# Issuing the first store behind a group of loads with 13 fields still outstanding

## Chip, core and metric

The kernel runs on one core of a Trainium2 chip. The metric is device time in microseconds for one execution of the whole program; lower is better.

## What is computed

For each of 4096 samples, x holds 32 fields of 64 numbers, and W is a 64 x 64 matrix. Each field is multiplied by W, and every pair of fields i < j (496 pairs) gives an elementwise product:

```python
vid = jnp.einsum('bfd,de->bfe', x, W)
F_ = x.shape[1]
idx_i, idx_j = jnp.triu_indices(F_, k=1)
return x[:, idx_i, :] * vid[:, idx_j, :]
```

All is 32-bit floating point. The output is 15 times as large as the input: the profile counts 33.59 MB read from HBM and 520.09 MB written to it.

## The kernel before

**Tiles.** Samples are split into 16 tiles of 256. A tile lies in on-chip memory with the 64 embedding numbers on the partitions, two halves of the samples on the lower and the upper 64 of them, and 32 fields of 128 samples along each partition. One field of a tile is thus 128 partitions x 512 bytes, 64 KB. On-chip memory is one tensor, `mem`, of 445 such fields, and both input tiles and outgoing products have places in it: `XPLACE` says where each tile lies, `SLOTS` the size and place of each of the 71 store buffers. Many places are used again and again, so a load or a product must wait until the store that reads the place has finished.

**Work on a tile.** TensorE computes `vid` for the 32 fields into PSUM (L173). VectorE multiplies the fields with broadcast fields of `vid` (L197), in blocks of pairs, and writes the products into the buffer of the moment. When a buffer is full, SP issues one DMA that stores it (L200).

**Loads.** Tile 0 comes first, in two DMAs (L137, L141). Then follow, at the head of the program, tiles 1 to 3 in one DMA and tiles 5 and 4 in two. Two more groups of five tiles each are loaded in the course of the program: tiles 6 to 10, and tiles 15 to 11. The loop asks for them when two loaded tiles are left. `GROUPS` names the tiles, `CUTS` the pieces into which a group's load is cut, as ranges of fields within it:

```python
CUTS = [[None, [(0, 32), (32, 64)]], [(0, 127), (127, 160)], [(33, 160), (0, 33)]]
```

**Order.** Everything that SP does stands in one queue, in the order in which the program names it; loads and stores alike go out on it. A DMA is cut into 128 rows, one for each partition, and these are spread over 16 DMA engines, eight rows to each.

**The extra wait.** `load` returns the list of DMAs of the pieces, and `pieces` holds the latest list. The first store that comes after a group of loads gets a dependency, set by `behind`, so that SP issues it only when an earlier piece has landed. With `pieces.pop(0)` this is the first piece of the list, which leaves 32 fields of load outstanding at the head and 33 in the two middle groups. After that store `pieces` is empty, and later stores wait for VectorE alone. This wait is no matter of correctness: the store reads other places than the load writes.

Of the kernel before, what the change touches and what calls it, by code (L numbers as in the profile page):

```python
# [21 lines left out]
    [[6, 7, 8, 9, 10]],  # L22
    [[15, 14, 13, 12, 11]],
]
CUTS = [[None, [(0, 32), (32, 64)]], [(0, 127), (127, 160)], [(33, 160), (0, 33)]]
XPLACE = [317, 349, 381, 413, 32, 0, 285, 317, 349, 381, 413, 128, 96, 64, 32, 0]


# [25 lines left out]
def by_block():  # L54


    def within(lo):
        yield "step", lo, 2, 1, 0
        for k in range(2):
            yield "step", lo, 4, 2, k  # L60
        for i in (lo, lo + 8):
            yield "row", i + 4, i, 4, 4
        yield "row", lo + 8, lo, 8, 8

    yield from within(0)
    yield "row", 16, 0, 16, 16
    yield from within(16)


def products(blocks, at=0):  # L70

    for kind, a, b, c, d in blocks:
        if kind == "row":
            rows, n, i0, di, j0, dj = c, d, b, 0, a, 1
        else:
            rows, n, i0, di, j0, dj = 16 // b, c, a, b, a + c + d, b
        r = k = 0
        while r < rows:
            room = BREAKS[bisect_right(BREAKS, at)] - at
            if k or room < n:  # L80
                m, w = 1, min(n - k, room)
            else:
                m, w = min(rows - r, room // n), n
            yield at, m, w, i0 + r * di + k, di, j0 + r * dj, dj
            at += m * w
            if k + w == n:
                r, k = r + m, 0
            else:
                k += w
# [10 lines left out]
@with_exitstack  # L100
def pairwise_bilinear_kernel(
    ctx: ExitStack,
    tc: tile.TileContext,
    x0: bass.AP,
    x: bass.AP,
    out: bass.AP,
):

    nc = tc.nc
    NT = sum(len(tiles) for group in GROUPS for tiles in group)
    F = x0.shape[1] - 1 - PAD0
    D = P // 2
    NP = F * (F - 1) // 2

    BANK = 512 // C


    ctx.enter_context(tc.manual_schedule(engines={mybir.EngineType.SP}))

    const = ctx.enter_context(tc.tile_pool(name="const", bufs=1))
    psum = ctx.enter_context(
        tc.tile_pool(name="ps", bufs=1, space=bass.MemoryType.PSUM)
    )
    vid = psum.tile([P, F, C], F32)

    mem = const.tile([P, UNITS, C], F32)  # L130


    w2 = const.tile([P, D], F32)


    place = XPLACE[0]
    nc.sync.dma_start(  # L137
        out=mem.rearrange("p u c -> p (u c)")[:, place * C - D : (place + F // 2) * C],
        in_=x0.rearrange("p u c -> p (u c)")[:, C - D : (1 + F // 2) * C],
    )  # L140
    nc.sync.dma_start(out=mem[:, place + F // 2 : place + F, :], in_=x0[:, 1 + F // 2 : 1 + F, :])  # L141
    nc.vector.tensor_copy(w2, mem[:, place - 1, C - D :])  # L142
    loaded = 1

    def load(tiles, cuts=()):
        nonlocal loaded
        n = len(tiles) * F
        place = XPLACE[tiles[0]]
        at = (loaded - 1) * F
        loaded += len(tiles)  # L150
        return [
            nc.sync.dma_start(out=mem[:, place + lo : place + hi, :], in_=x[:, at + lo : at + hi, :])  # L152
            for lo, hi in cuts or [(0, n)]
        ]

    ready = mybir.DependencyInfo(mybir.DependencyClass.Sync, mybir.DependencyReason.DATA)

    def behind(later, earlier):
        tc.add_manual_dep(later.ins, earlier.ins.name, ready, reason="issued when that has landed")

    pieces = []
    groups, cuts = iter(GROUPS), iter(CUTS)
    for tiles, parts in zip(next(groups)[1:], next(cuts)):
        pieces = load(tiles, parts)

    for t in range(NT):
        xt = mem[:, XPLACE[t] : XPLACE[t] + F, :]


        for b in range(0, F, BANK):  # L170
            for h in range(2):
                half = slice(h * D, (h + 1) * D)
                nc.tensor.matmul(  # L173
                    vid[half, b : b + BANK, :],
                    lhsT=w2[half, :],
                    rhs=xt[half, b : b + BANK, :],
                    start=True,
                    stop=True,
                )

        for at, m, w, i, di, j, dj in products(by_block(), t * NP):
            slot = bisect_right(STARTS, at) - 1
            n = m * w
            begin, end = STARTS[slot], STARTS[slot + 1]
            ot = mem[:, SLOTS[slot][1] : SLOTS[slot][1] + SLOTS[slot][0], :]
            o = ot[:, at - begin : at - begin + n, :]
            if m == 1:
                left = xt[:, i : i + w, :]
                right = vid[:, j : j + 1, :].to_broadcast([P, w, C])
            else:  # L190
                o = o.rearrange("p (m w) c -> p m w c", m=m)
                right = vid[:, j : j + (m - 1) * dj + 1 : dj, :].unsqueeze(2).to_broadcast([P, m, w, C])
                if di == 0:
                    left = xt[:, i : i + w, :].unsqueeze(1).to_broadcast([P, m, w, C])
                else:
                    left = xt.rearrange("p (m d) c -> p m d c", d=di)[:, i // di : i // di + m, i % di : i % di + w, :]
            nc.vector.tensor_tensor(o, left, right, ALU.mult)  # L197
            at += n
            if at == end:
                store = nc.sync.dma_start(out=out[:, begin:end, :], in_=ot)  # L200
                if pieces:
                    behind(store, pieces.pop(0))
                    pieces.clear()


        if t + 2 == loaded < NT:
            (tiles,) = next(groups)
            pieces = load(tiles, next(cuts))
# [45 lines left out]
```

## Time and profile before

| | |
|---|---|
| median of three runs | 1288.03 us (1287.9 to 1288.14) |
| profiled execution, its own time | 1287.86 us |
| its span, first to last instruction | 1286.1 us |
| VectorE busy with products (L197) | 1091.0 us, 455 instructions |
| TensorE busy (L173) | 220.7 us, 512 instructions |
| VectorE idle, waiting for stores | 154.9 us |
| TensorE idle, waiting for loads | 89.5 us, three times |
| stores (L200) | 71; 19.7 to 41.7 us from issue to landing, median 25.5 |
| loads of groups (L152) | 7; 21.3 to 44.3 us from issue to landing, median 37.8 |

The span is what the profile shows; the execution's own time has 1.76 us around it. The shares of busy time are averages, and busy time of an engine that isn't the bound costs nothing. In a list of waits a line reads: who waited, for whom, microseconds in total, times, longest. In a table of windows each line is a stretch of time, the busy time of TensorE's multiplications, its weight loads, VectorE and GpSimd with the number of their instructions, the clock granted to TensorE, the DMA engines' busy share, and GB/s. There a row of a transfer is counted where it starts, so the rates of short stretches scatter.

### The profile page before, as it was taken

Reading aid. Unit: us, or ns where it says so; the run is one execution under the profiler, and the core shown is the slowest. Engines: PE = TensorE matmul, PEld = TensorE weight load, DVE = VectorE, ACT = ScalarE, POOL = GpSimd, SP = SyncE. Lnnn points to the kernel's source line nnn. Section 1 sums busy time; section 2 is a strip of 40 time slices with the busy share of each in tenths; the row PEclk is TensorE's granted clock in tenths of the full one; section 3 lists DMA queues with packets and bytes.
Section 4 is the critical chain, followed back from the end, with each engine's and each line's share of the span. In section 5 each row is a group of like instructions: output and inputs, shape, how many; then the busy total and the mean of one; then the engine's idle time right before and its main releaser. Section 6 shows DMA issues by size and latency. Waiting matters only on the chain.

```text
span 1286.1 us, 1756 instructions
## 1 busy us (share of the span) xinstructions
PE 220.7 (17%) x512; PEld 40.5 (3%) x512; DVE 1091.2 (85%) x456; POOL 0.2 (0%) x4
## 2 busy tenths in 40 slices
PE   4031221303110113030311211103121120212000
PEld 1000000000000000000000000000000000000000
DVE  6899979988995489998998995649999799999952
POOL 0000000000000000000000000000000000000000
PEclk8555565555555656555655655555555565656555
DMA  9999999999999999999999999999999999999998
GB/s 385 434 433 440 442 424 443 431 437 428 432 442 421 441 425 433 434 441 428 434 433 443 426 437 427 417 443 428 431 434 445 423 441 435 421 447 421 445 423 376
DMA packets 11529, 553.79 MB, mean 431 GB/s; under 512 B 1280, under 2 KB 1280, under 8 KB 1280
## 3 DMA queue, kind: packets, MB, share of 16 engines
q1 hardware_dynamic: 11520, 553.69, 99.7%
q8 instruction: 4, 0.07, 0.0%
q14 instruction: 5, 0.04, 0.0%
HBM read 33.59 MB, written 520.09 MB: 431 GB/s over the span
## 4 chain that ended last, share of the span: by engine, by line
DMA 48%; DVE 47%; issue 3%; PE 0%; DVEq 0%; SPq 0%
DVE mem L197 47%; DMA out_dram<-mem 44%; DMA mem<-in_r_x_dram 3%; PE vid L173 0%; DVEq L242 0%; DVEq L197 0%; SPq L200 0%; DVE w L142 0%; SPq L152 0%
## 5 line engine op out<-in xcount | busy, mean ns | idle before, releaser
L197 DVE TENSOR_TENSOR mem<-mem,vid 128x1024 f32<-128x1024 f32 (+16 forms) x455 | 1091.0, 2471 | 164.8 <-DMA out_dram<-mem 154.9
L173 PE MATMUL vid<-mem,w 64*64 64x512 f32 x512 | 220.7, 985 | 963.3 <-DVE mem L197 867.7
L173 PEld LDWEIGHTS vid<-mem,w 64*64 64x64 f32 x512 | 40.5, 196 | 1141.9 <-DVE mem L197 1010.5
L142 DVE COPY w<-mem 128x64 f32<-128x64 f32 x1 | 0.2, 195 | 5.9 <-DMA mem<-in_r_x_dram 5.9
L222 POOL MEMSET const-bfloat16-1.0<- 128x1 bf16 x1 | 0.1, 101 | 0.0
L222 POOL MEMSET const-uint8-127<- 128x1 uint8 x1 | 0.1, 101 | 0.0
L222 POOL MEMSET const-float32-0.0<- 128x1 f32 x1 | 0.1, 98 | 0.2 <-issue 0.2
L222 POOL MEMSET const-float32-1.0<- 128x1 f32 x1 | 0.1, 98 | 0.0
## 6 DMA issues: line engine op xcount, KB each, us to landing
out_dram<-mem SPq DMA_DIRECT2D x21, 8128.0 KB, 26.7
out_dram<-mem SPq DMA_DIRECT2D x13, 7936.0 KB, 28.4
out_dram<-mem SPq DMA_DIRECT2D x3, 7424.0 KB, 24.8
out_dram<-mem SPq DMA_DIRECT2D x3, 6656.0 KB, 22.4
out_dram<-mem SPq DMA_DIRECT2D x3, 6144.0 KB, 21.0
out_dram<-mem SPq DMA_DIRECT2D x3, 5888.0 KB, 23.9
out_dram<-mem SPq DMA_DIRECT2D x3, 5440.0 KB, 24.6
mem<-in_r_x_dram SPq DMA_DIRECT2D x2, 8128.0 KB, 38.1
```

Source lines behind the costliest of these rows:

```text
L142: nc.vector.tensor_copy(w2, mem[:, place - 1, C - D :])
L173: nc.tensor.matmul(vid[half, b : b + BANK, :], lhsT=w2[half, :], rhs=xt[half, b : b + BANK, :], start=True, stop=True,)
L197: nc.vector.tensor_tensor(o, left, right, ALU.mult)
L222: nc = _bacc.Bacc("TRN2", target_bir_lowering=False, num_devices=1, dynamic_dma_scratch_size=1024)
```

## The change

The groups' loads are cut differently. The head's two pieces are 51 and 13 fields instead of 32 and 32. The middle groups are loaded in three pieces instead of two: 127, 20 and 13 fields, and the same sizes counted from the other end for the last group. The first store behind a group of loads waits for the last piece but one, so that 13 fields are outstanding when it is issued. What is loaded, where it goes, and all the computation stay as they are.

```diff
-CUTS = [[None, [(0, 32), (32, 64)]], [(0, 127), (127, 160)], [(33, 160), (0, 33)]]
+CUTS = [[None, [(0, 51), (51, 64)]], [(0, 127), (127, 147), (147, 160)], [(33, 160), (13, 33), (0, 13)]]
...
                 store = nc.sync.dma_start(out=out[:, begin:end, :], in_=ot)
                 if pieces:
-                    behind(store, pieces.pop(0))
+                    behind(store, pieces[-2])
                     pieces.clear()
```

## The prediction

> **What bounds the kernel now.** I read the page from the top, then SP's own waits, SP's timeline around the loads, and the rates in windows. The page first:
>
> ```profile
> span 1286.1 us, 1756 instructions
> PE 220.7 (17%) x512; PEld 40.5 (3%) x512; DVE 1091.2 (85%) x456; POOL 0.2 (0%) x4
> ...
> DMA  9999999999999999999999999999999999999998
> ...
> q1 hardware_dynamic: 11520, 553.69, 99.7%
> ...
> HBM read 33.59 MB, written 520.09 MB: 431 GB/s over the span
> ```
>
> The 16 DMA engines are busy in every slice, so the transfers bound the kernel. Section 4's chain gives 47% to VectorE, but it ends in stores and each VectorE stretch in it lies beside a full queue: VectorE itself waits 154.9 us for stores to free their buffers. A microsecond that an engine of the DMA loses is therefore a microsecond of the end, if that engine is the last one. SP's waits show where the change acts:
>
> ```profile
> SPq L200 <- DVE mem L197: 1109.7, 67, 34.7
> SPq L200 <- DMA mem<-in_r_x_dram: 97.6, 3, 36.9
> ```
>
> Of 71 stores (L200), three wait for a load. They are these, each the first store row behind a row of loads (L152) in SP's timeline:
>
> ```profile
> 1.62 1.65 SPq L152 DMA_DIRECT2D mem<-in_r_x_dram  x3
> 27.90 15.13 SPq L200 DMA_DIRECT2D out_dram<-mem  x2
> ...
> 382.50 1.56 SPq L152 DMA_DIRECT2D mem<-in_r_x_dram  x2
> 420.32 0.82 SPq L200 DMA_DIRECT2D out_dram<-mem  x2
> ...
> 790.47 1.64 SPq L152 DMA_DIRECT2D mem<-in_r_x_dram  x2
> 829.05 2.72 SPq L200 DMA_DIRECT2D out_dram<-mem  x2
> ```
>
> At the head, the rate of the transfers falls once that store has been issued (last column, GB/s):
>
> ```profile
> 22.50:29.00 6.50, 5.28 (x14) 1.41 (x16) 6.50 (x5) 0.00 (x0) 0.61 0.99 423
> 29.00:32.50 3.50, 0.80 (x4) 0.00 (x0) 3.50 (x1) 0.00 (x0) 0.78 1.05 290
> ...
> 100.00:380.00 280.00, 52.13 (x112) 8.19 (x108) 260.94 (x114) 0.00 (x0) 0.52 1.00 435
> ```
>
> 290 instead of 423 GB/s, with the engines busy all the time: the last load packets run slower while the store is queued behind them. The packet records say the same: rows of 16 KB take 0.61 us until 29.1 us and up to 1.48 us after it, and the store's rows follow each engine's last load row about 10 ns later. There is no hole now.
>
> What the view can't show is how far the 16 engines are apart. I took it from the 16 completion updates of each transfer. All engines carry the same rows, but at the end the first is done at 1281.78 us and the last at 1285.27 us. The last engine sets the time.
>
> **What the Trainium skill says.** "DMA: Bandwidth & Descriptors", section "Queues, rings and completion order": an issuing sequencer has one ring on each of 16 engines, consumed in order. The trace agrees (10 ns from row to row, store after load). The same page, "Why a DMA increments its semaphore by 16 and not by 1": only the full 16 means that all has landed. The trace agrees: the first load at 382.50 landed on its engines from 418.21 to 420.27 us, and the waiting store went out at 420.32. The same page, "Specifications", gives 0.6 us from issue to the first byte on this path. The trace shows more: the first load is issued at 0.73 and its rows start, engine by engine, from 1.72 to 2.41 us, so 1.0 to 1.7 us. I use the trace.
>
> **The change part by part.** Call L the time from SP's issue of the store to its first row. It is not seen on a drained queue. From below, the start of the program shows 1.0 us. The slowdown sets in 1.2 us after the issue at the head, and 1.4 us at 829.05. From above: at 420.32 the first engine out of load rows started the store's row at 422.88 without a hole, so at most 2.55 us. I take 1.5 and keep 1.1 and 2.55 for the range.
>
> *Two more transfers.* The middle groups are loaded in three pieces instead of two; the head keeps its number. From the medians of rows (16,384 B 0.611 us, 8,192 B 0.309 us), a row costs 0.007 us plus its bytes at 27.1 GB/s, and a 0.01 us gap. Eight more rows per engine are 0.14 us, twice 0.28 us, on the path. SP's own issue (0.34 to 1.25 us for one) hides in its 37 us wait.
>
> *Who waits.* Behind the waiting store stand only stores: at 420.72 (already computed) and 831.43, and at the head one at 42.69. The wait grows by 19 fields at the head, some 3 us, and by 20 in the middle; the queue is full in that time. TensorE's data comes with the untouched first piece in the second group (127 fields) and the third (33 to 160); tile 4, split at the head, is used far later. VectorE waits for landings of stores, which move with the queue. No cost, and what little it is late (0 to 1 us) VectorE's 165 us of idle time covers.
>
> *The tail.* After the wait, 13 fields are left: 8 x (0.007 + 6,656 B / 27.1 GB/s + 0.01) = 2.1 us, against 5.0 us now. From landing to issue takes 0.05 to 0.08 us, and a row's end to its landing 0.34 us. So the store comes 0.4 + L = 1.9 us behind the slowest engine's last row of the piece, just before its tail is over (2.1). A slowest engine has no hole while L stays below 1.7. A faster one has: its lead + 1.9 - 2.1.
>
> *Head.* The two pieces land on the slowest engine at 27.82 and 34.08: 6.26 us for 8 x 0.622 = 4.98, so 1.28 lost; the mean (27.34 to 33.48) loses 1.16. After: the slowest ends its loads at 34.08 - 1.28 - 0.34 = 32.46; the store comes at 32.46 - 2.1 + 1.9 = 32.26. Engines are only 0.8 apart here. Gain 1.25 us for the slowest, about 0.8 for the mean.
>
> *First middle join.* Slowest 420.27 to 426.27: 6.00 for 8 x 0.64 = 5.12, 0.88 lost. Mean 418.86 to 423.98: nothing lost, only late engines are hit. After: 420.27 - 1.25 + 5.12 + 0.14 - 0.34 = 423.94 is the slowest's end, and the store starts on every engine at 423.7 to 423.9. Now they start it from 422.88 to 425.99, mean 423.6. The slowest gains 2.05 in all, but the leads of the others, up to 3.1 us, are gone: they wait for the slowest, as at a barrier.
>
> *Second.* Those leads matter, because single engines are held up: comparing the updates of successive stores, one engine loses 1.44 us near 167, one 1.45 near 489, one 1.96 near 788 (and gets 0.53 back), one 1.76 near 1115 us, and none of the last three was the slowest. With leads gone, such a loss counts in full. An undelayed engine takes 403.78 us from the first join to the next load (423.24 to 827.02, the first updates); from 423.94 + 0.34 this gives 828.06, and with 1.43 of delay 829.5, against 828.99 now. Loads end at 829.5 + 5.12 + 0.14 - 0.34 = 834.4 and all start there; now from 831.71 to 834.92. Gain left: 0.5 us.
>
> *To the end.* Undelayed 449.69 us (832.09 to 1281.78). From 834.4 + 0.34: 1284.43. The engine that loses 1.76 gains some 1.3 on the mean: 1285.7, against 1285.27. **Sum: +0.4 us**, so the profiled execution goes from 1287.86 (span 1286.1 and 1.76 around it) to 1288.3. The median is 0.17 above that execution: 1288.4.
>
> The same sum engine by engine with L = 1.1 ends at -0.9, with 2.0 at +1.6, with 2.55 at +3.2 us.
>
> **Rivals.**
> 1. *Slow rows gone, leads not needed.* If delays belong to fixed slow engines, or fall on engines with room, the slowest saves 1.28 + 0.88 + 1.09 (828.99 to 835.20 is 6.21 for 5.12) - 0.28 = 3.0: 1285.1. For it: the engine last at 835 is still last at the end. Against: the engines delayed near 489, 788 and 1115 were others.
> 2. *A hole at each join.* With L near 2.5, even the slowest engine stands idle for 0.4 + 2.5 - 2.1 = 0.8 us at each of three joins, and the faster ones 2 to 3 us more, so that their later delays count in full: +3.2, 1291.2. For it: at 420.32 no row slowed before 2.4 us after issue. Against: 1.2 to 1.4 us at the other two. It decides from L = 2.3 on, at two or three joins.
> 3. *The slowdown belongs to the change of direction itself*, and hits the last load rows wherever the store is issued; 13-field rows are then slowed as the larger were, and only the two transfers count: 1288.3 + small holes, 1288.6. Against: onset follows the issue, not the end of the loads.
>
> **How the numbers follow.** Forecast 0.62, rival one 0.12, rival two 0.20, rival three 0.06. About 0.2%, or 2.6 us (1285.5 to 1290.6), is what a measurement of this kernel can tell from no change. Rival one lies mostly below it, so faster 0.10; rival two mostly above it, and a little of the forecast's upper bound, so slower 0.20; same 0.70. The range runs from part of rival one to rival two: 1285.9 to 1291.3.
>
> **What would show it.** Load rows keep their 0.61 us equivalent to the last one at the head, and the rate from 29 to 32.5 stays near 423. Two more DMA issues at L152. First stores at about 30.8, 422 and 832 us. The first rows of these stores start on all engines within 1 us of each other, with holes on the fast engines of 2 us in the middle. Wrong if the slow rows remain, if the engines keep their leads through the joins, or if the store's rows start over 2 us after its issue.

## The result, and the profile after

The changed kernel takes 1290.41 us (median of 18 runs, 1289.72 to 1290.73) against 1288.08 (18 runs, 1287.77 to 1288.55): ratio 1.0018, interval 1.001 to 1.0025. It is slower by 2.3 us, just inside the 0.2% that the forecast had called no change. The page of the kernel after:

```profile
span 1288.6 us, 1763 instructions
PE 222.7 (17%) x512; PEld 40.5 (3%) x512; DVE 1091.2 (85%) x456; POOL 0.2 (0%) x4
...
DMA  9999999999999999999999999999999999999998
...
q1 hardware_dynamic: 11808, 553.69, 99.7%
q8 instruction: 4, 0.07, 0.0%
q14 instruction: 5, 0.04, 0.0%
...
HBM read 33.59 MB, written 520.09 MB: 430 GB/s over the span
```

The same work, the same bytes, 288 packets more (two transfers of 144), and still 99.7% of the DMA engines' time: a page that averages can't show where 2.5 us of span went. SP's waits and its timeline show that the change does what it says:

```profile
SPq L200 <- DVE mem L197: 1100.7, 66, 32.4
SPq L200 <- DMA mem<-in_r_x_dram: 106.3, 3, 40.2
```

```profile
30.57 11.71 SPq L200 DMA_DIRECT2D out_dram<-mem  x2
...
381.48 2.94 SPq L152 DMA_DIRECT2D mem<-in_r_x_dram  x3
423.58 44.91 SPq L200 DMA_DIRECT2D out_dram<-mem  x4
...
791.24 2.95 SPq L152 DMA_DIRECT2D mem<-in_r_x_dram  x3
834.45 33.60 SPq L200 DMA_DIRECT2D out_dram<-mem  x3
```

Three loads stand in each middle group, and the three stores wait longer: 106.3 us instead of 97.6. Windows of the kernel after, the head first, then the last microsecond or so before the store's rows in the middle (last two columns: the DMA engines' share and GB/s, with rows counted where they start):

```profile
22.50:29.00 6.50, 5.48 (x16) 1.38 (x16) 6.50 (x5) 0.00 (x0) 0.71 0.99 426
29.00:32.50 3.50, 0.04 (x2) 0.00 (x0) 3.50 (x1) 0.00 (x0) 1.00 1.27 541
...
423.30:424.40 1.10, 1.10 (x5) 0.26 (x4) 0.00 (x0) 0.00 (x0) 0.50 0.29 121
...
833.60:835.20 1.60, 1.60 (x6) 0.52 (x4) 0.00 (x0) 0.00 (x0) 0.51 0.30 121
```

The same two middle windows of the kernel before:

```profile
423.30:424.40 1.10, 1.10 (x6) 0.27 (x4) 0.00 (x0) 0.00 (x0) 0.91 0.78 330
833.60:835.20 1.60, 1.12 (x6) 0.15 (x2) 0.00 (x0) 0.00 (x0) 1.00 1.57 682
```

At the head the dip is gone. In the middle there is one now: most of the 16 engines have finished their loads and stand idle until the store comes. The packet records agree. At the head every load row keeps its 0.25 us and the store's rows follow without a hole from 31.52 us. In the middle 15 engines start the store together at 424.42 to 424.60, although most were out of loads by 423.8.

The 16 completion updates of a transfer give a ledger. The first number is the mean over the engines, the second the last engine:

```
landed                      before              after           after - before
first store             49.80    50.38      48.57    48.85      -1.23   -1.53
22nd store             399.77   401.10     399.73   400.19      -0.04   -0.91
second group's loads   423.98   426.27     424.15   425.49      +0.17   -0.78
store behind them      438.49   440.82     439.46   440.06      +0.97   -0.76
45th store             808.32   809.37     809.97   810.39      +1.65   +1.02
third group's loads    833.05   835.20     834.60   836.37      +1.55   +1.17
store behind them      852.25   854.44     855.00   855.58      +2.75   +1.14
last store            1282.77  1285.27    1286.44  1287.68      +3.67   +2.41
```

The mean column adds up to the loss. The head gives 1.23 us. The 21 stores behind it take 1.19 back. The two joins in the middle, where a store follows a group's loads, cost 0.80 and 1.20; by the rows, an engine stands idle there for 0.7 and 1.1 us on the mean, so these are the holes. The long stretches behind them cost 0.68 and 0.92. The stretches that end with the loads add 0.21 and take 0.10 off. In return the last engine is only 1.24 us behind the mean at the end, not 2.50, and 3.67 becomes 2.41. Holes were forecast. That plain stores, far from any join, take longer was not: the experiments had to say whether that is real.

### The profile page after: what moved, and what is told of

Same layout as the page of the kernel before. It is cut to its first block, busy times and chain, and to the rows that moved or that the text cites. A ratio compares the mean times of both kernels' runs of the same rounds, so it can differ in the third digit from the quotient of the medians.

```text
span 1288.6 us, 1763 instructions
## 1 busy us (share of the span) xinstructions
PE 222.7 (17%) x512; PEld 40.5 (3%) x512; DVE 1091.2 (85%) x456; POOL 0.2 (0%) x4
## 3 DMA queue, kind: packets, MB, share of 16 engines
q1 hardware_dynamic: 11808, 553.69, 99.7%
## 4 chain that ended last, share of the span: by engine, by line
DMA 52%; DVE 43%; issue 3%; PE 0%; DVEq 0%; SPq 0%
DMA out_dram<-mem 45%; DVE mem L197 42%; DMA mem<-in_r_x_dram 7%; PE vid L173 0%; DVEq L242 0%; SPq L152 0%; SPq L200 0%; DVEq L197 0%; DVE w L142 0%
## 5 line engine op out<-in xcount | busy, mean ns | idle before, releaser
L197 DVE TENSOR_TENSOR mem<-mem,vid 128x1024 f32<-128x1024 f32 (+16 forms) x455 | 1091.0, 2471 | 167.4 <-DMA out_dram<-mem 158.1
```

## The experiments

Each is a cut of the groups (`CUTS`) or of the wait. Each comparison is with runs of the kernel before on the same chip (medians 1287.95 to 1288.09).

**The head alone.**

```diff
-CUTS = [[None, [(0, 51), (51, 64)]], [(0, 127), (127, 147), (147, 160)], [(33, 160), (13, 33), (0, 13)]]
+CUTS = [[None, [(0, 51), (51, 64)]], [(0, 127), (127, 160)], [(33, 160), (0, 33)]]
```

> The head's new cut (51 and 13 fields) with the middle groups cut and waited for as before. Theory 1 (the head gains, the middle joins lose): the first store lands about 1.5 us earlier on the slowest engine, and the end is 0.5 to 1.3 us earlier than before, 1286.8 to 1287.6. Rival (engines that run in step are slower, and the head is what puts them in step): the gain at the head is used up by the end of the first stretch, and the time is 1288 to 1289.

1287.98 us, ratio 1.0000 (0.9992 to 1.0008). The first store lands 1.46 us earlier on the last engine, and 1.27 on the mean, but the 22nd store only 0.07 on the mean. The rival's outcome holds: the gain is real and gone by 400 us. Its reason accounts for about half of that; the other half is told below, under what the sum lacked.

**The middle alone.**

```diff
-CUTS = [[None, [(0, 51), (51, 64)]], [(0, 127), (127, 147), (147, 160)], [(33, 160), (13, 33), (0, 13)]]
+CUTS = [[None, [(0, 32), (32, 64)]], [(0, 127), (127, 147), (147, 160)], [(33, 160), (13, 33), (0, 13)]]
```

> The middle groups cut in three and waited for as after the change, the head as before. Theory 1: the loss of the change and the head's gain on top, +3.0 to +4.0 us, 1291.1 to 1292.1. Rival (the head causes the loss): +1 us at most.

1289.92, ratio 1.0014 (1.0007 to 1.002). The loss sits in the middle, but it is +1.9, not 3 to 4: I had added a gain of the head that doesn't last.

**The finer cut without the later wait.**

```diff
-CUTS = [[None, [(0, 32), (32, 64)]], [(0, 127), (127, 160)], [(33, 160), (0, 33)]]
+CUTS = [[None, [(0, 32), (32, 64)]], [(0, 127), (127, 147), (147, 160)], [(33, 160), (13, 33), (0, 13)]]
```

> The middle groups cut in three, but the store waits for the first piece as before, so that 33 fields are outstanding. It prices the two transfers more. Theory 1: +0.3 us (0.14 each), 1288.4. Rival (the finer cut is what costs): +2 us or more.

1288.29, ratio 1.0002 (0.9993 to 1.001), so the rival's +2 us is excluded. From the first piece to the last, the fastest engine takes 5.12 and 5.10 us instead of 5.03 and 5.07: 0.03 to 0.09 us for a transfer more, rather less than the 0.14 of the sum.

**In step, without touching a load.** Engines are called in step here when they work on the same row of a transfer within a fraction of a microsecond of each other. To the kernel before, with `stores` a list of the stores issued so far:

```diff
                     pieces.clear()
+                elif len(stores) == 24:
+                    behind(store, stores[-1])
+                stores.append(store)
```

> The kernel before, with one store in the middle (the 25th) that waits until the store before it has landed. No cut and no load is changed; it empties the queue once near 460 us and so brings all engines into step there. If engines in step lose 0.05 us per store, the mean over the engines from that store to the next group's loads takes 0.4 to 0.6 us longer than before (314.63 us from the landing of the 25th to that of the 44th store), and the end is 3.3 to 4 us later. If being in step costs nothing, that stretch is the same within 0.1 us, and the end is 2.2 to 3 us later, by the hole and the leads that are lost.

1291.74, ratio 1.0028 (1.0017 to 1.0038): +3.7 us for one emptied queue. Its windows show the hole; in the kernel before, the first of them has 485 GB/s:

```profile
456.00:459.80 3.80, 0.00 (x0) 0.00 (x0) 0.00 (x0) 0.00 (x0) 0.50 0.04 17
459.80:460.70 0.90, 0.00 (x0) 0.00 (x0) 0.81 (x2) 0.00 (x0) 0.50 0.75 319
460.70:478.00 17.30, 2.95 (x8) 0.58 (x8) 16.27 (x6) 0.00 (x0) 0.50 1.04 448
```

All engines start within 0.14 us (460.69 to 460.83), and the store lands with 0.19 us between the first and the last, against 3.15 before. The stretch to the 44th store then takes 315.02 us on the mean instead of 314.63: 0.39 more, just under the 0.4 to 0.6 that was expected, and outside the 0.1 of the other theory. No load and no cut was touched in it. Behind the third group's loads the engines of this run are 3.2 us apart again, and its last 24 stores take 411.80 us, exactly as before. The other runs sort the same way; next to each other (one profiled execution of each), the stretch from the 25th to the 44th store, and from the 47th to the last:

```
                          apart at the start   25th to 44th   apart at the start   47th to last
before                          3.15              314.63             3.21              411.80
head alone                      2.64              314.27             2.90              411.80
finer cut, old wait             3.11              314.53             2.91              411.76
after                           0.58              315.00             0.65              412.66
middle alone                    0.52              315.00             0.86              412.61
emptied once                    0.19              315.02             3.17              411.80
```

Where the engines are less than 1 us apart, the first stretch takes 0.4 us more and the second 0.8 to 0.9, in all five cells; where they are over 2.6 us apart, neither does. That is some 0.02 to 0.035 us per store on the mean, and the profile names no wait for it. Three limits belong to this table. The kernel before has one transfer of instructions more in the first stretch (at 771 us, see below), which is worth 0.1 us of its 314.63, so 0.4 is rather 0.5. The loss is not even: it is 0.02 to 0.08 us for each of the first ten to sixteen stores behind the wait and mostly 0.02 or less for the later ones. And 1 us is no border: at the head, where the engines are 0.93 us apart before the change and 0.57 after it, the 2nd to 5th stores take the same time within 0.02 us, and with 0.20 us (the run with five fields outstanding, below) they take 0.03 to 0.05 us more each. So it is shown that stores behind a wait that has lined up the engines are slower; why, and why that fades, is not.

**Five fields outstanding**, at all three places.

```diff
-CUTS = [[None, [(0, 51), (51, 64)]], [(0, 127), (127, 147), (147, 160)], [(33, 160), (13, 33), (0, 13)]]
+CUTS = [[None, [(0, 59), (59, 64)]], [(0, 127), (127, 155), (155, 160)], [(33, 160), (5, 33), (0, 5)]]
```

> 5 fields outstanding instead of 13 at all three places. The hole theory: the tail of a load is 8 rows of 5 fields, 0.9 us, instead of 2.1, so every engine stands idle some 1.2 us longer at each place: +3 to +4 us on the changed kernel, 1293.4 to 1294.4, with about 0.4 us of hole even on the slowest engine. If holes on engines don't reach the end: the same as the changed kernel, 1290.4.

1294.09, ratio 1.0048 (1.0032 to 1.0063): 3.7 us above the changed kernel, as the hole theory had it. Its two stretches, begun with the engines 0.19 and 0.15 us apart, take 315.02 and 412.70 us, as slow as those of the changed kernel. In two windows of this run nearly all of the 16 engines stand:

```profile
424.90:426.60 1.70, 1.70 (x8) 0.61 (x6) 0.00 (x0) 0.00 (x0) 0.65 0.08 33
836.50:838.50 2.00, 2.00 (x6) 0.52 (x4) 0.00 (x0) 0.00 (x0) 0.50 0.04 17
```

**Twenty-four fields outstanding in the middle**, 13 at the head.

```diff
-CUTS = [[None, [(0, 51), (51, 64)]], [(0, 127), (127, 147), (147, 160)], [(33, 160), (13, 33), (0, 13)]]
+CUTS = [[None, [(0, 51), (51, 64)]], [(0, 127), (127, 136), (136, 160)], [(33, 160), (24, 33), (0, 24)]]
```

> 24 fields outstanding in the middle, 13 at the head; still three pieces. The tail lasts 3.8 us, and the store comes about 1.2 us behind the slowest engine's piece, so that an engine up to 2.5 us ahead has no hole. The hole theory: the stores' first rows follow the loads without a hole on nearly all engines, the engines keep their leads (spread over 2 us at the store behind), and the time is 1288 to 1288.6, as with the head's cut alone and two transfers more. If the wait for the last piece but one itself is what costs: 1290 as with 13.

1287.61, ratio 0.9997 (0.9989 to 1.0005), 0.4 us below what the hole theory had: the loss of the change is gone with 11 fields more, and the wait on the last piece but one is not what costs. The two windows have no dip:

```profile
423.30:424.40 1.10, 1.10 (x4) 0.25 (x4) 0.00 (x0) 0.00 (x0) 0.50 1.49 603
833.60:835.20 1.60, 1.60 (x8) 0.59 (x6) 0.00 (x0) 0.00 (x0) 0.65 1.49 640
```

The engines keep leads of 2.91 and 2.31 us at the stores behind the loads. The first stretch takes 314.49 us, as without the change. The last takes 412.35, between the two groups of the table, with 2.24 us between the first and the last engine at its start; so here too the distance between these two isn't the whole measure.

**No wait at all**, in the kernel before.

```diff
                 if pieces:
-                    behind(store, pieces.pop(0))
                     pieces.clear()
```

> The kernel before without the wait: the first store behind a group of loads goes out as soon as VectorE has filled its buffer. If a store that is queued behind loads slows their rows from about 1 us after its issue on, as at the head, the loads in the middle take several us longer and the end is 3 to 15 us later. If only the engines that still load while others store are slowed, the wait is worth little and the time is 1287.5 to 1289.

1288.71, ratio 1.0005 (0.9996 to 1.0013), so at most 1.7 us and not told from nothing; that is the second of the two forecasts. With the engines 3.00 and 2.78 us apart, its two stretches take 314.51 and 411.59 us. The store behind the second group is issued at 402.57, 18 us earlier, and the loads don't care until their last rows. This kernel:

```profile
402.60:417.80 15.20, 0.00 (x0) 0.00 (x0) 15.20 (x5) 0.00 (x0) 0.50 0.96 415
...
421.00:424.50 3.50, 3.50 (x10) 0.94 (x8) 1.33 (x1) 0.00 (x0) 0.50 1.12 391
```

and the kernel before, in which the store is issued at 420.32:

```profile
402.60:417.80 15.20, 0.00 (x0) 0.00 (x0) 15.20 (x5) 0.00 (x0) 0.50 0.96 415
...
421.00:424.50 3.50, 3.50 (x12) 0.98 (x10) 1.25 (x1) 0.00 (x0) 0.64 1.13 471
```

415 GB/s in both while the loads run, with a store queued behind them or not. The first slow rows come at 421.0, when an engine has some three of its 8 rows of the last piece left. At the head they begin at 29.07 with the store issued at 26.30, and at 29.09 with the store issued at 27.90. So slow rows belong to the last two to four rows of a load with a store already queued behind it, and not to a time after the store's issue. How many there are differs: in the kernel before, 4 of the 128 rows ahead of the store issued at 420.32 took over 0.72 us (median 0.63), and 17 ahead of the one issued at 829.05.

**Two pieces again, 24 fields outstanding**, with the head's new cut and with its old one.

```diff
-CUTS = [[None, [(0, 51), (51, 64)]], [(0, 127), (127, 147), (147, 160)], [(33, 160), (13, 33), (0, 13)]]
+CUTS = [[None, [(0, 51), (51, 64)]], [(0, 136), (136, 160)], [(24, 160), (0, 24)]]
```

> 24 fields outstanding in the middle and 13 at the head, but the middle groups in two pieces (136 and 24 fields), so that no transfer is added. If a transfer more costs 0.14 us: 0.3 us less than with three pieces, 1287.3, and with that 0.7 us less than before. TensorE gets its first tile 9 fields, about 1.4 us, later, which VectorE's wait for a buffer covers.

1287.52, ratio 0.9997 (0.9989 to 1.0005), 0.1 us from the run with three pieces and not the 0.3 that was expected: a transfer more can't be told at this size.

> The same middle (136 and 24 fields), with the head's old cut (32 fields outstanding). If the head's gain is used up by engines that then run in step, this one is within 0.3 us of the run with the head's new cut, 1287.3. If the head's gain lasts, it is about 1 us slower than that run, 1288.3.

1287.21, ratio 0.9995 (0.9986 to 1.0003). With the head's old cut it is 0.3 us below the run with the new one, so the head's gain does not last. It is the lowest median of all, 0.7 us below the kernel before, but the interval holds 1: it is not shown to be faster. In these two runs the engines are 2.19 and 2.30 us apart at the start of the first stretch, which takes 314.66 and 314.27 us, and 2.38 and 2.28 at the start of the second, which takes 412.28 and 412.32: the first as without the change, the second between the two groups, like the run with three pieces.

## Why the prediction held, and where its steps didn't

*The outcome.* Inside the range, and no change beyond 0.2% was the likeliest case; the direction was right, and the +0.4 us too small by 2 us. The result is nearer to the second rival's 1291.2 than to the forecast, yet not by that rival's mechanism: L is not near 2.5, and the slowest engine has no hole at either join. The first rival (leads not needed, 1285.1) is refuted: the 0.80 and 1.20 us of the joins are still in the mean of the ledger at the end. Stage by stage, the store's rows in the middle were forecast to start at 423.8 and 834.4 us, and the last store to end at 1285.7; measured, the rows start at 424.5 and 835.4 on the mean, and the end is at 1287.7. So the sum fell behind by 0.7 us up to the first join, by 0.3 to the second, and by 1.0 from there to the end.

*L, the mis-sized term.* I took 1.5 us from issue to the first row, with 1.1 as the lower end. It is 0.84 us in the middle (423.58 to 424.42, 834.45 to 835.29), and 0.84 on a queue that was wholly empty (459.85 to 460.69 in the run that empties it). At the head 0.95 us went by, but there the first row follows straight behind a load row, so that it gives no more than an upper bound. The lower end came from the start of the program, where another transfer's delay bounds nothing from below, and from the slow rows. The second was a misreading: with no wait the slow rows at the head come at the same time although the store was issued 1.6 us earlier, and in the second group not until 18 us after the issue. "Onset follows the issue", which I held against the third rival, is refuted; that rival's own claim, that they come wherever the store is issued, is refuted too, since a store that comes when the loads are all but over leaves no slow row (no load row of 13 fields took over 0.28 us in the kernel after; their median is 0.25).

*The head.* Forecast -1.25 us on the slowest engine and -0.8 on the mean; measured -1.53 and -1.23. Right in kind, and of no use: what it brings is lost in the next 21 stores, and the sum carried it on to the first join.

*The joins as barriers.* Right. The leads, up to 3.1 us, shrink to 0.7, and fast engines wait. The landing-to-issue time (0.06 to 0.08 us) and the tail of 2.1 us held. The hole is 0.7 and 1.1 us on the mean, and not the 2 us that the fast engines were to have, since L is shorter.

*Delays of single engines count in full.* Only in part. The profile has a name for the four delays: they coincide with transfers of instructions. The Trainium skill, "Runtime: NRT & Kernel Launch", section "Instruction fetch mechanics", says that each engine's instruction memory is refilled in blocks of 16 KiB through a DMA queue of its own; the traces agree in the size (16,384 B), and show what such a block costs the store stream. The window from 481 to 484 us of the kernel before:

```profile
q1 hardware_dynamic: 28, 1.22, 94.6%
q8 instruction: 1, 0.02, 2.0%
```

The page has four of these on q8, 16 KB each. In the kernel before they start at 150.78, 482.27, 771.43 and 1102.08 us, and the delayed engines show at the completions near 169, 489, 788 and 1117. After the change, three lie at 149.77, 481.90 and 1118.49, and one engine falls 1.8 to 2.0 us behind the mean at each; the fourth, at 834.00, falls into the hole. The delay goes with the transfer: in the nine runs in which the one of 771 us comes at 832 to 838 instead, the 44th store takes 0.10 to 0.15 us less on the mean than in the kernel before, about what 1.96 us on one engine of 16 are worth, and in the run without a wait, where it stays at 772, no less.

Such a delay shrinks again, though. After the change the 26th store, behind the transfer at 481.90, lands with 2.17 us between the first and the last engine, and the 44th with 1.15; behind the transfer at 1118.49 the last engine is 2.00 us behind the mean, and 1.24 at the end (forecast: some 1.3). And the engine that all wait for at the second join is not one that a transfer of instructions has delayed: at the 45th store all 16 are within 0.74 us, and then one load row, begun at 809.89 us, takes 4.30 us where their median is 2.40. The packets carry no engine's number, but this fits the one update that comes 1.8 us behind the mean when that load lands.

*What the sum lacked.* The recorded sums fall with L, from +3.2 us at 2.55 to -0.9 at 1.1. With the measured 0.84 they would have forecast a gain of more than 0.9 us, which is an estimate along these sums, where the last engine lost 2.4. That the forecast had the right sign is therefore luck: an L that was too long stood in for costs that the sum had at nothing.

Two of these costs are shown. One is the slower pace behind the waits, 0.68 and 0.92 us in the two long stretches and about half (0.6) of the 1.19 behind the head, spread over 20 stores. The other half of the 1.19 falls on one store, the 22nd, behind which the next loads are queued: it takes 19.55 us on the mean after and 18.95 before. Its packet records show why: in the kernel after, 14 of the 16 engines need 2.9 to 3.4 us for their last row of it, where a row takes 2.35 otherwise; in the kernel before, two need 2.7 and the others less. It is 14 in all five runs with 13 or 5 fields outstanding at the head, where these 14 rows begin within 0.20 to 0.35 us of each other, and 2 to 4 in the other six, where the first 14 begin within 1.1 to 1.4 us. So it is not only load rows ahead of a queued store that are slowed, but also store rows ahead of a queued load; at this place it went with how close together the engines came to it. The terms found are 2.8 us on the mean, less than what separates the corrected sum from the measurement; the rest is not assigned.

Nothing in the profile of before had shown engines less than some 0.8 us apart, and I had assumed that a queue kept full has one pace. The Trainium skill, "DMA: Bandwidth & Descriptors", section "Queues, rings and completion order", has each engine drain its own ring in order; the traces agree (without a hole, the waiting store's rows follow each engine's last load row after about 10 ns), but show besides that the pace isn't the same in all stretches of a full queue (315.00 against 314.63 us for 19 stores).

*Two transfers.* Sized at 0.28 us; 0.06 to 0.18 from the completions, and not told from nothing by the times.

*TensorE and VectorE.* No cost, as forecast. VectorE waits 158.1 us for stores instead of 154.9: 3.2 us more, no more than the queue's own delay (3.67 us on the mean at the end).

*Left open.* Why stores behind a wait are slower, and what slows the last rows ahead of a queued transfer of the other direction. An experiment that brings engines out of step without giving some of them more rows wasn't tried.

## What to carry to other kernels

A store or load that waits for a completion waits for the slowest of 16 engines; the work left in the queue at that moment must last through the fastest engine's lead plus the issue, not only through the issue. Here 2.1 us of work against 1.3 us of issue (0.34 from a row's end to its landing, 0.07 to the issue, 0.84 to the first row) and leads of 1.4 to 2 us made holes, and 3.8 us made none. A hole that touches only engines that are ahead is no free hole either: its 0.80 and 1.20 us were still in the mean at the end, and behind a wait that lined up the engines, this kernel's stores were slower.

## What the runs showed of the hardware that was not expected

- From issue to first row, a store took 0.84 us where the engines had run dry (423.58 to 424.42, 834.45 to 835.29, 459.85 to 460.69); the first load of the program took 1.0 to 1.7, engine by engine.
- Sixteen engines that began within 0.65 us of each other, behind a wait, took 315.00 us for 19 stores and 412.66 for 24; engines that began 3 us apart took 314.63 and 411.80.
- One instruction fetch of 16 KB, 0.88 to 0.96 us in its own record in the kernels before and after, put one engine 1.4 to 2.0 us behind, and part of that was made up again (2.17 us between first and last engine at the 26th store, 1.15 at the 44th).
- A store queued for 18 us behind loads changed nothing in them (415 GB/s with and without) up to the last two to four rows of each engine, which took up to 2.1 us instead of 0.63.
- The last rows of a store with a load queued behind it took 2.9 to 3.4 us instead of 2.35 on 14 engines that began them within 0.29 us of each other (22nd store, after), and at most 2.7 where the first 14 began within 1.11 us (before).
